# Moving step-size, read-out and copy instructions to other places in a scan loop that runs background work in slots

## The chip, the cores and the metric

The kernel runs on one core of a Trainium2 chip. Its engines are TensorE (PE in the profile, PEld for its weight loads), VectorE (DVE), ScalarE (ACT), GpSimd (POOL) and SyncE (SP), which issues all of the kernel's DMAs. Each engine works through its own list of instructions in order and waits for the others by semaphores. The metric is the device time of one execution in microseconds, and the median of several runs is compared.

## The reference, cut to what matters

Two residual layers work on 16 images of 64 x 64 pixels and 96 channels. The first layer upsamples by Fourier filters, applies a small network with a quadratic in the middle, and downsamples again. The second layer is a selective scan in four directions. Its core, per direction, is this recurrence over 4096 positions for 192 channels and 16 states each:

```python
delta = jax.nn.softplus(dts + dt_bias[None, :, :, None])
def step(h, inps):
    dt, ut, bt, ct = inps
    h = jnp.exp(dt[..., None] * As[None]) * h + (dt * ut)[..., None] * bt[:, :, None, :]
    y = jnp.einsum('bkdn,bkn->bkd', h, ct)
    return (h, y)
...
x = x + _L0_conv_ref(_gn(x), ...)
x = x + _L1_conv_ref(_gn(x), ...)
```

Both layers normalise their input by groups of channels over the whole image. Around the scan the second layer has a 3 x 3 convolution, projections that make `dt`, B and C, a layer norm, a gate and an output projection.

## The kernel before

**The loop.** `scan()` walks through 3072 units `(step, block, j)`: 16 images, 8 steps each (four stretches of T = 1024 positions forward with directions 0 and 1, then four backward with directions 2 and 3), 6 blocks per step (`blocks`, `bi` 0 to 5: 64 channels of one direction each), and 4 values of `j` (four states each). A tile has 32 channels x 4 states on its 128 partitions and 1024 positions along the free axis. A unit holds two such tiles, called odd (e = 1) and even (e = 0).

In each unit:

- ScalarE makes the decays, `da = exp(delta * A)`, in PSUM (`decay`, L821), one unit ahead.
- GpSimd makes `b = dtu * B` for both tiles (`drive`, L827), two units ahead.
- VectorE runs the recurrence of the odd tile, then of the even tile (`recur`, L836 forward and L838 backward), then multiplies the even states by C (L988).
- The odd states are multiplied by C on GpSimd (L977) for j = 0 to 2, and on VectorE (L968) for j = 3 (`odd_here`).
- `keep` (L844) copies the last state of each tile for the next stretch.
- TensorE sums over the states (`read_out`, L861, eight matmuls), one unit late: at unit n it reads out unit n-1. The result `y` gathers the four units of a block in one PSUM bank. In the backward half of an image, `y` begins with the forward part, fetched from DRAM and added by L853.
- After the last unit of a block, `store` copies `y` to SBUF on ScalarE (L872) and, one unit later, issues its DMA.

**Slots.** The order on each engine is written out by hand. Each unit calls `slot(0)`, `slot(1)` and `slot(2)` between its own instructions. A slot advances two generators by one piece: `work`, made by `block_work` for the block, and the background, if it is due. A block has 12 such places, p = 0 to 11, with p = 3j + position.

**The background** is `front(mi + 1)`, everything of the next image ahead of its scan, and after it `finish(mi - 1)`, everything of the last image behind its scan. A `Background` is due while its pieces so far are fewer than `at * SLICES / POS`, where POS = 576 is the number of places in an image. `front` says `WAIT` ahead of the activations that change ScalarE's table; they are then put into position 2 of a unit with j = 2. `norm` is called twice by `front`.

**The step sizes.** `block_work` also runs, once per block, a `task`. It makes 512 positions of `delta` and `dtu` for a later block. Its pieces in order are: fetch `u`, and a matmul into `s` (L683); Abs and Exp on ScalarE (L686, L687); Relu and `1 + e` (L689, L690); Ln (L692); `1 - w` (L694); one empty place; four matmuls that sum `w`, `e`, `d` and `m`, into `s` (L699); two or three empty places; `dtu = s * u` on VectorE (L703); a copy of `s` into `delta` on ScalarE (L705) and the DMA of `dtu` (L706); the DMA of `delta` (L708). Tasks in blocks 3 and 4 have `late = 1`: they begin one place later and make it up before L703, so the product is at place 9 in every block. In blocks 2 and 3 `block_work` also fetches three tiles of `u` at p = 6 and mixes them on TensorE at p = 11 (`mix`, L661); `mixed` turns the result into `pr` on ScalarE (L666) and stores its rows by DMA (L668) at p = 0 of the next block. `s` and `pp` share one PSUM bank, the only buffer of the pool `gps`. Of `y` there is one buffer, of `da` one per parity, of `b` four, of `u` four.

Of the kernel before, what the change touches and what calls it, by code (L numbers as in the profile page):

```python
# [64 lines left out]
NQ = 4  # L65
QT = T // NQ
TB = 512
# [1 line left out]
NEPS = 1e-5  # L69
BOTH = "natural_log_exp_and_others"  # L70
POS = 3 * 8 * 6 * NQ
SLICES = 540
FINISH = 117
WAIT = -1

# [2 lines left out]
def tile_two_blocks(  # L78
# [4 lines left out]
    nc = tc.nc  # L83
# [116 lines left out]
    def norm(xt):  # L200

        s = small.tile([C, 8], F32, name="gs")
        for t in range(8):
            junk = piece([C, TB], "junk")
            nc.scalar.activation(junk, xt[:, TB * t:TB * t + TB], AF.Identity, accum_out=s[:, t:t + 1])
            if t % 2:
                yield
        yield
        m_ps = bank([C, 8], "m_ps")
        nc.tensor.matmul(m_ps, lhsT=gmask_s, rhs=s, start=True, stop=True)  # L210
        yield
        junk8 = small.tile([C, 8], F32, name="junk8")
        nmean = small.tile([C, 1], F32, name="nmean")
        nc.scalar.activation(junk8, m_ps, AF.Identity, scale=-1.0, accum_out=nmean)
        s2 = small.tile([C, 8], F32, name="gs2")
        for t in range(8):
            junk = piece([C, TB], "junk")
            nc.scalar.activation(
                junk, xt[:, TB * t:TB * t + TB], AF.Square, bias=nmean, accum_out=s2[:, t:t + 1]
            )  # L220
            if t % 2:
                yield
        yield
        v_ps = bank([C, 8], "v_ps")
        nc.tensor.matmul(v_ps, lhsT=gmask_s, rhs=s2, start=True, stop=True)
        yield
        var = small.tile([C, 1], F32, name="var")
        nc.scalar.activation(junk8, v_ps, AF.Identity, accum_out=var)
        rg = small.tile([C, 1], F32, name="rg")
        nc.scalar.activation(var, var, AF.Ln, bias=eps_g[0:C])  # L230
        nc.scalar.activation(rg, var, AF.Exp, scale=-0.5)
        nb = small.tile([C, 1], F32, name="nb")
        nc.scalar.activation(nb, nmean, AF.Identity, scale=rg)
        yield
        yield
        return rg, nb
# [389 lines left out]
    def scan():  # L626


        with ExitStack() as es:
# [21 lines left out]
            def fetch_u(st, v, t):  # L651
                mi, _, lc = steps[st]
                uv = up_.tile([128, TB], F32, name="u")
                nc.sync.dma_start(out=uv, in_=image[mi]["xs"][v, :, lc * T + t:lc * T + t + TB])
                return uv

            def mix(st, us, ps):
                pair = steps[st][1]
                pp = ps.tile([128, TB], F32, name="pp", tag="g")
                for v in range(3):  # L660
                    nc.tensor.matmul(pp, lhsT=xpt_s[:, pair, v, :], rhs=us[v], start=(v == 0), stop=(v == 2))  # L661
                return pp

            def mixed(st, t, pp):
                pr = prp.tile([128, TB], F32, name="pr")
                nc.scalar.activation(pr, pp, AF.Identity, bias=bumps_s)  # L666
                for r in range(2):
                    nc.sync.dma_start(  # L668
                        out=ctxs[st]["rows"][r, :, t:t + TB], in_=pr[64 * r:64 * r + 2 * NS, :]
                    )  # L670
                ctxs[st]["pr"][t] = pr

            def task(st, k, ps, make, late=0):

                v, t = tasks[k]
                ctx, pair = ctxs[st], steps[st][1]
                u = fetch_u(st, v, t)
                for _ in range(late):  # L680
                    yield
                s = ps.tile([128, TB], F32, name="s", tag="g")
                nc.tensor.matmul(s, lhsT=dtw_s[:, pair, v, :], rhs=ctx["pr"][t], start=True, stop=True)  # L683
                yield
                e, d, m, w = (make(k) for k in ("e", "d", "m", "w"))
                nc.scalar.activation(e, s, AF.Abs)  # L686
                nc.scalar.activation(e, e, AF.Exp, scale=-1.0)  # L687
                yield
                nc.scalar.activation(m, s, AF.Relu)  # L689
                nc.scalar.activation(w, e, AF.Identity, bias=one_s)  # L690
                yield
                nc.scalar.activation(d, e, AF.Ln, bias=one_s)  # L692
                yield
                nc.scalar.activation(w, w, AF.Identity, scale=-1.0, bias=one_s)  # L694
                yield
                yield
                s = ps.tile([128, TB], F32, name="s", tag="g")
                for i, of in enumerate((w, e, d, m)):
                    nc.tensor.matmul(s, lhsT=ident_s, rhs=of, start=(i == 0), stop=(i == 3))  # L699
                for _ in range(3 - late):  # L700
                    yield
                dtu, delta = make("dtu"), make("delta")
                nc.vector.tensor_mul(dtu, s, u)  # L703
                yield
                nc.scalar.copy(delta, s)  # L705
                nc.sync.dma_start(out=ctx["dtu"][v][:, t:t + TB], in_=dtu)  # L706
                yield
                nc.sync.dma_start(out=ctx["delta"][v][:, t:t + TB], in_=delta)  # L708

            def near(name):  # L710
# [2 lines left out]
            def block_work(st, bi, mi):  # L713
                more = st + 1 < len(steps)
                work = iter(())
                if bi < 3:
                    work = task(st, bi + 3, gps, near)
                elif more:
                    work = task(st + 1, bi - 3, gps, near, 1 if bi < 5 else 0)
                for p in range(3 * NQ):  # L720
                    if p == 0 and more and bi in (3, 4):
                        mixed(st + 1, *mixing.pop())
                    next(work, None)
                    if more and bi in (2, 3):
                        if p == 6:
                            if bi == 2:
                                if steps[st + 1][0] > mi:
                                    ahead_gen.drain()
                                open_step(st + 1)
                            us = [fetch_u(st + 1, v, TB * (bi - 2)) for v in range(3)]  # L730
                        elif p == 11:
                            mixing.append((TB * (bi - 2), mix(st + 1, us, gps)))
                    yield

            def spread(out, what, ctx, bi, e):
# [33 lines left out]
            units = [(si_, bi, j) for si_ in range(len(steps)) for bi in range(len(blocks)) for j in range(NQ)]  # L769
# [37 lines left out]
            gps = es.enter_context(tc.tile_pool(name="sc_gps", bufs=1, space=PSUM))  # L807
# [10 lines left out]
            def decay(n, e):  # L818
                k, g = group(n, e)
                da = aps.tile([128, T], F32, name="da", tag=f"da{e}")  # L820
                nc.scalar.activation(da, deltas[n // NQ, e], AF.Exp, scale=a_s[:, k, g, units[n][2]:units[n][2] + 1])  # L821
                das[n, e] = da
# [88 lines left out]

            nothing = Background(None, 0, 1)
            ahead_gen = behind_gen = nothing
            work, mixing = iter(()), []

            def slot(position):
                back = ahead_gen if ahead_gen.gen is not None else behind_gen
                if back is behind_gen and back.at == 0:
                    back.positions = 3 * (per_image - n % per_image) - 6
                back.at += 1  # L920
                next(work, None)
                if back.due() and (back.said != WAIT or (position == 2 and units[n][2] == NQ - 2)):
                    back.step()
# [6 lines left out]
            storing = None  # L930

            for n, (st, bi, j) in enumerate(units):
# [11 lines left out]
                if j == 0:  # L944
                    work = block_work(st, bi, mi)
# [15 lines left out]
                odd_here = j == NQ - 1  # L961
                h = das[n, 1] if odd_here else bs[n][:, 1, :]
                recur(n, 1, h)
                if not odd_here:
                    decay(n + 1, 1)
                slot(0)
                if odd_here:
                    nc.vector.tensor_mul(bs[n][:, 1, :], h, bc[1, r, j])  # L968
# [3 lines left out]
                if storing is not None:  # L972
                    next(storing, 0)
                    storing = None
# [7 lines left out]
                recur(n, 0, h)  # L982
                if not odd_here:
                    keep(n, 1, states_of_odd, nc.vector.tensor_copy)
                if n >= 1:
                    read_out(n - 1)
                slot(1)
                nc.vector.tensor_mul(bs[n][:, 0, :], h, bc[1, r, j])  # L988
                keep(n, 0, h, nc.scalar.copy)
                if n < last:  # L990
                    decay(n + 1, 0)
                if n >= 1 and units[n - 1][2] == NQ - 1:
                    storing = store(n - 1)
                    next(storing)
                slot(2)
                if j == NQ - 1 and n < last and steps[units[n + 1][0]][1] == 1:
                    st2, bi2, _ = units[n + 1]
# [124 lines left out]
```

## Time and profile before

| | |
|---|---|
| median of the runs shown | 20482.93 us |
| lowest and highest | 20482.35, 20484.85 us |
| the profiled execution's own time | 20473.08 us |
| its span | 20471.3 us |
| granted clock of TensorE, mean | 0.873 |
| DMA engines' mean busy share in the loop, bytes per second | 0.66, 223 GB/s |
| L836 and L838, one scan with a carried state | 2340 to 2342 ns |
| L821, one decay | 1118 ns |
| L703, product of step size and u | 680 ns |
| L705, copy of delta | 579 ns |
| L872, copy of y | 579 ns |

The span is the time from the first instruction to the last of one profiled execution. A group's line gives the source line, the engine, the operation with what it writes and reads, the shapes, the count, the busy time, the mean duration of one, and the idle time just before them with what ended it. A line of waits gives who waited for whom, the total, the number of waits, and the longest. In a timeline, the first column is the start and the second the duration, both in us, and idle time stands in brackets at the end.

### The profile page before, as it was taken

Reading aid. Unit: us, or ns where it says so; the run is one execution under the profiler, and the core shown is the slowest. Engines: PE = TensorE matmul, PEld = TensorE weight load, DVE = VectorE, ACT = ScalarE, POOL = GpSimd, SP = SyncE. Lnnn points to the kernel's source line nnn. Section 1 sums busy time; section 2 is a strip of 40 time slices with the busy share of each in tenths; the row PEclk is TensorE's granted clock in tenths of the full one; section 3 lists DMA queues with packets and bytes.
Section 4 is the critical chain, followed back from the end, with each engine's and each line's share of the span. In section 5 each row is a group of like instructions: output and inputs, shape, how many; then the busy total and the mean of one; then the engine's idle time right before and its main releaser. Section 6 shows DMA issues by size and latency. Waiting matters only on the chain. (4 is left out here: it accounts for less than half of the span.)

```text
span 20471.3 us, 274485 instructions
## 1 busy us (share of the span) xinstructions
PE 16699.0 (82%) x98988; PEld 7171.0 (35%) x98988; DVE 19208.3 (94%) x12989; ACT 13815.5 (67%) x20694; POOL 19150.8 (94%) x5384
## 2 busy tenths in 40 slices
PE   7877888888888878788887888888887787888767
PEld 4423334343333433334233343433334333242222
DVE  0999999999999999999999999999999999999997
ACT  4676767667676776766767676676767767677554
POOL 0999999999999999999999999999999999999996
PEclk8888898988889889888888889888898888888888
DMA  2666666766667676666766667667676666766664
GB/s 85 212 224 208 223 234 211 242 214 222 231 218 239 210 240 220 217 235 214 235 218 221 234 215 238 218 220 234 217 237 210 234 223 216 238 217 232 221 214 157
DMA packets 1966064, 4478.55 MB, mean 219 GB/s; under 512 B 461726, under 2 KB 560958, under 8 KB 1962654
## 3 DMA queue, kind: packets, MB, share of 16 engines
q1 hardware_dynamic: 1964702, 4461.00, 64.5%
q8 instruction: 781, 12.80, 0.3%
q14 instruction: 581, 4.76, 0.1%
HBM read 3581.91 MB, written 878.18 MB: 218 GB/s over the span
## 5 line engine op out<-in xcount | busy, mean ns | idle before, releaser
L827 POOL TENSOR_TENSOR b<-dtu,bt 128x2048 f32<-128x2048 f32 x3072 | 13903.4, 4538 | 471.7 <-DMA dtu<-dtu_d 467.9
L821 ACT ACTIVATE da<-delta,a_s 128x1024 f32<-128x1024 f32 x6144 | 6868.4, 1118 | 2264.3 <-DVE b L988 849.7
L977 POOL TENSOR_TENSOR odd<-b,ct 128x1024 f32<-128x1024 f32 x2304 | 5456.2, 2368 | 679.3 <-DVE b L836 246.2
L988 DVE TENSOR_TENSOR b<-da,ct 128x1024 f32<-128x1024 f32 x3072 | 3760.5, 1224 | 41.8
L836 DVE TENSOR_TENSOR_SCAN da<-da,new,b 128x1024 f32<-128x1024 f32 x1440 | 3372.8, 2342 | 82.6 <-ACT da L821 78.9
L838 DVE TENSOR_TENSOR_SCAN da<-da,new,b 128x1024 f32<-128x1024 f32 x1440 | 3370.2, 2340 | 15.8 <-ACT da L821 14.7
L861 PE MATMUL y<-b,fold_s 128*32 128x256 f32 x30720 | 2561.2, 427 | 797.7 <-ACT yt L872 411.5
L844 ACT COPY new<-da 128x1 f32<-128x1 f32 x2880 | 457.1, 159 | 2434.9 <-DVE b L988 1892.3
L836 DVE TENSOR_TENSOR_SCAN b<-da,new,b 128x1024 f32<-128x1024 f32 x864 | 2023.8, 2342 | 29.3 <-ACT da L821 28.3
L838 DVE TENSOR_TENSOR_SCAN b<-da,new,b 128x1024 f32<-128x1024 f32 x864 | 2022.5, 2341 | 29.2 <-ACT da L821 29.2
L487 PE MATMUL c_ps<-xgp,wtap_s 96*64 96x512 f32 (+1 forms) x4608 | 1764.7, 640 | 77.7 <-ACT row L505 71.9
L861 PEld LDWEIGHTS y<-b,fold_s 128*32 128x32 f32 x30720 | 739.7, 114 | 2919.4 <-issue 1557.0
L861 PE MATMUL y<-odd,fold_s 128*32 128x256 f32 x18432 | 1599.9, 421 | 197.3 <-POOL odd L977 197.0
L683 PE MATMUL s<-pr,dtw_s 128*128 128x512 f32 x1536 | 1034.5, 761 | 689.9 <-ACT delta L705 574.0
L661 PE MATMUL pp<-u,xpt_s 128*128 128x512 f32 x1536 | 891.7, 726 | 461.4 <-ACT delta L705 319.1
L699 PE MATMUL s<-w,ident_s 128*128 128x512 f32 x1534 | 1054.0, 775 | 238.4 <-ACT w L694 211.5
L370 PE MATMUL h_ps<-xu,w1t_s 96*128 96x500 f32 x1920 | 1038.8, 642 | 166.1 <-ACT hsq L351 121.1
L836 DVE TENSOR_TENSOR_SCAN da<-da,b 128x1024 f32<-128x1024 f32 x480 | 1096.2, 2284 | 79.2 <-ACT da L821 75.1
L838 DVE TENSOR_TENSOR_SCAN da<-da,b 128x1024 f32<-128x1024 f32 x480 | 1095.2, 2282 | 10.7 <-ACT da L821 9.2
L382 PE MATMUL o_ps<-w2c_s,hsq 128*100 128x96 f32 x9600 | 1009.2, 263 | 71.6 <-ACT hsq L351 71.3
L382 PEld LDWEIGHTS o_ps<-w2c_s,hsq 128*100 128x100 f32 x9600 | 946.0, 176 | 266.2 <-ACT hsq L351 111.4
L487 PEld LDWEIGHTS c_ps<-xgp,wtap_s 96*64 96x64 f32 (+1 forms) x4608 | 631.8, 177 | 1081.2 <-issue 942.6
(140 smaller groups left out, 23002.7 us busy)
## 6 DMA issues: line engine op xcount, KB each, us to landing
dtu<-dtu_d SPq DMA_DIRECT2D x1536, 512.0 KB
delta<-delta_d SPq DMA_DIRECT2D x1536, 512.0 KB
bt<-rows SPq DMA_DIRECT2D x1024, 512.0 KB
ct<-rows SPq DMA_DIRECT2D x1024, 512.0 KB
u<-xs_d SPq DMA_DIRECT2D x1664, 256.0 KB
dtu_d<-dtu SPq DMA_DIRECT2D x767, 256.0 KB
delta_d<-delta SPq DMA_DIRECT2D x767, 256.0 KB
xr<-in_x SPq DMA_DIRECT2D x768, 128.0 KB
```

The source lines that it names most:

```text
L370: nc.tensor.matmul(h_ps[j], lhsT=w1t_s[:, 128 * j:128 * (j + 1)], rhs=xu.rearrange("c p q -> c (p q)"), start=True, stop=True,)
L382: nc.tensor.matmul(o_ps[:, p, :], lhsT=hsq[j][:, UPS * p:UPS * (p + 1)], rhs=w2c_s[:, j, :], start=(j == 0), stop=(j == HB - 1),)
L487: nc.tensor.matmul(c_ps[p:p + n], lhsT=wtap_s[:, tap, 128 * i:128 * i + n], rhs=xgp[:, h0:h0 + 8, dx:dx + HW], start=(tap == 0), stop=(tap ...
L683: nc.tensor.matmul(s, lhsT=dtw_s[:, pair, v, :], rhs=ctx["pr"][t], start=True, stop=True)
L699: nc.tensor.matmul(s, lhsT=ident_s, rhs=of, start=(i == 0), stop=(i == 3))
L821: nc.scalar.activation(da, deltas[n // NQ, e], AF.Exp, scale=a_s[:, k, g, units[n][2]:units[n][2] + 1])
L827: nc.gpsimd.tensor_mul(b, dtus[n // NQ], bt.unsqueeze(1).to_broadcast([128, 2, T]))
L836: nc.vector.tensor_tensor_scan(out, da, b, before, ALU.mult, ALU.add)
L838: nc.vector.tensor_tensor_scan(out[:, ::-1], da[:, ::-1], b[:, ::-1], before, ALU.mult, ALU.add)
L861: nc.tensor.matmul(y[32 * q:32 * q + 32, e, :], lhsT=fold_s, rhs=weighed[e][:, QT * q:QT * q + QT], start=(pair == 0 and j == 0 and e == 0 ...
L977: nc.gpsimd.tensor_mul(odds[n], h, bc[1, r, j])
L988: nc.vector.tensor_mul(bs[n][:, 0, :], h, bc[1, r, j])
```

## The change

- In `task`, `late` is gone. The four sums (L699) follow directly behind the piece with L694, at place 5, and four empty places stand between them and the product at place 9. The copy into `delta` stands in the same piece as the product; both DMAs stand together in the next piece.
- In `block_work`, the three `u` are fetched at p = 3, mixed at p = 10, and `mixed` is called at p = 11 of the same block.
- `read_out(n - 1)` stands ahead of `slot(0)` for j = 0 to 2. For j = 3 it stays behind the even scan.
- The first half of `store`, with the copy of `y`, stands behind `slot(1)`, ahead of the even product, the even `keep` and the even decay. Its DMA stays in the next unit.
- `norm` hands back after each of its activations, not after every second one. SLICES is 570, not 540.

```diff
-SLICES = 540
+SLICES = 570
...
             nc.scalar.activation(junk, xt[:, TB * t:TB * t + TB], AF.Identity, accum_out=s[:, t:t + 1])
-            if t % 2:
-                yield
+            yield
...
-            def task(st, k, ps, make, late=0):
+            def task(st, k, ps, make):
...
                 u = fetch_u(st, v, t)
-                for _ in range(late):
-                    yield
...
                 nc.scalar.activation(w, w, AF.Identity, scale=-1.0, bias=one_s)
                 yield
-                yield
                 s = ps.tile([128, TB], F32, name="s", tag="g")
                 for i, of in enumerate((w, e, d, m)):
                     nc.tensor.matmul(s, lhsT=ident_s, rhs=of, start=(i == 0), stop=(i == 3))
-                for _ in range(3 - late):
+                for _ in range(4):
                     yield
                 dtu, delta = make("dtu"), make("delta")
                 nc.vector.tensor_mul(dtu, s, u)
-                yield
                 nc.scalar.copy(delta, s)
+                yield
                 nc.sync.dma_start(out=ctx["dtu"][v][:, t:t + TB], in_=dtu)
-                yield
                 nc.sync.dma_start(out=ctx["delta"][v][:, t:t + TB], in_=delta)
...
-                    work = task(st + 1, bi - 3, gps, near, 1 if bi < 5 else 0)
+                    work = task(st + 1, bi - 3, gps, near)
                 for p in range(3 * NQ):
-                    if p == 0 and more and bi in (3, 4):
-                        mixed(st + 1, *mixing.pop())
                     next(work, None)
                     if more and bi in (2, 3):
-                        if p == 6:
+                        if p == 3:
...
                             us = [fetch_u(st + 1, v, TB * (bi - 2)) for v in range(3)]
+                        elif p == 10:
+                            pp = mix(st + 1, us, gps)
                         elif p == 11:
-                            mixing.append((TB * (bi - 2), mix(st + 1, us, gps)))
+                            mixed(st + 1, TB * (bi - 2), pp)
...
                 if not odd_here:
                     decay(n + 1, 1)
+                if n >= 1 and not odd_here:
+                    read_out(n - 1)
                 slot(0)
...
-                if n >= 1:
+                if n >= 1 and odd_here:
                     read_out(n - 1)
                 slot(1)
+                if n >= 1 and j == 0:
+                    storing = store(n - 1)
+                    next(storing)
                 nc.vector.tensor_mul(bs[n][:, 0, :], h, bc[1, r, j])
                 keep(n, 0, h, nc.scalar.copy)
                 if n < last:
                     decay(n + 1, 0)
-                if n >= 1 and units[n - 1][2] == NQ - 1:
-                    storing = store(n - 1)
-                    next(storing)
                 slot(2)
```

More of the change, by code (lines that the diff above doesn't have):

```diff
@@ L220, in norm @@
             )
-            if t % 2:
-                yield
+            yield
         yield
@@ L703, in task @@
                 nc.vector.tensor_mul(dtu, s, u)
+                nc.scalar.copy(delta, s)
                 yield
-                nc.scalar.copy(delta, s)
                 nc.sync.dma_start(out=ctx["dtu"][v][:, t:t + TB], in_=dtu)
-                yield
                 nc.sync.dma_start(out=ctx["delta"][v][:, t:t + TB], in_=delta)
@@ L913, in scan @@
             ahead_gen = behind_gen = nothing
-            work, mixing = iter(()), []
+            work = iter(())
             def slot(position):
```

## The prediction

> **What bounds the kernel now.** I read the page's busy shares first, then its costliest groups.
>
> ```profile
> span 20471.3 us, 274485 instructions
> ...
> PE 16699.0 (82%) x98988; PEld 7171.0 (35%) x98988; DVE 19208.3 (94%) x12989; ACT 13815.5 (67%) x20694; POOL 19150.8 (94%) x5384
> ...
> L827 POOL TENSOR_TENSOR b<-dtu,bt 128x2048 f32<-128x2048 f32 x3072 | 13903.4, 4538 | 471.7 <-DMA dtu<-dtu_d 467.9
> ...
> L977 POOL TENSOR_TENSOR odd<-b,ct 128x1024 f32<-128x1024 f32 x2304 | 5456.2, 2368 | 679.3 <-DVE b L836 246.2
> L988 DVE TENSOR_TENSOR b<-da,ct 128x1024 f32<-128x1024 f32 x3072 | 3760.5, 1224 | 41.8
> ```
>
> VectorE and GpSimd share the loop. It lasts from the first scan at 473.6 us to 20307.9, 19834 us for 768 blocks of four units. VectorE is busy 19183 us of it and idle 651. How far this can fall shows in two windows, images 14 and 15; the last runs no `front` for a following image.
>
> ```profile
> 17868.50:19108.00 1239.50, 1028.38 (x6186) 443.48 (x6186) 1199.93 (x811) 861.55 (x1294) 1197.08 (x337) 0.89 0.67 226
> 19108.00:20308.00 1200.00, 795.52 (x3945) 267.53 (x3944) 1194.55 (x801) 688.10 (x980) 1187.82 (x335) 0.78 0.59 205
> ```
>
> The columns are window, length, then PE, PEld, DVE, ACT and POOL busy. VectorE does the same work in both, but idles 40 us in the first and 5 in the second. So GpSimd doesn't hold the loop above 1200 us, and about 15 x 40 = 600 us are to be had. The waits of VectorE say from whom:
>
> ```profile
> DVE dtu L703 <- PE s L699: 455.1, 226, 159.9
> ...
> DVE da L836 <- ACT da L821: 154.0, 149, 3.5
> DVE b L838 <- ACT da L821: 88.2, 73, 2.4
> ```
>
> Of the 455, one wait of 159.9 lies ahead of the loop and a few more belong to it. Stepping through the timeline I count 286 us inside the loop, 236 of them (168 waits) in blocks 3 and 4, where `late=1`. The scans wait 322 us; 261 is the time by which a decay (L821) ended after VectorE was free: even scan of unit 1: 76; odd scan of unit 0: 67; even scan of unit 2: 60; odd scan of unit 2: 36; even scan of unit 3: 20. One of the stalled blocks on the merged timeline:
>
> ```profile
> 4616.15 1.08 PE L861 MATMUL y<-b,fold_s 128*32 128x256 f32 x8
> 4616.21 2.35 DVE L836 TENSOR_TENSOR_SCAN da<-da,new,b 128x1024 f32<-128x1024 f32 x1
> ...
> 4617.92 1.12 PE L699 MATMUL s<-w,ident_s 128*128 128x512 f32 x2
> ...
> 4620.60 1.02 PE L699 MATMUL s<-m,ident_s 128*128 128x512 f32 x2
> ...
> 4621.66 0.69 DVE L703 TENSOR_TENSOR dtu<-s,u 128x512 f32<-128x512 f32 x1 [3.10 <-PE s L699]
> ...
> 4623.24 0.56 ACT L310 COPY t<-o_ps 100x480 f32<-100x480 f32 x1 [5.60 <-PE o_ps L382]
> ...
> 4625.93 0.58 ACT L705 COPY delta<-s 128x512 f32<-128x512 f32 x1
> ```
>
> The four sums take 3.7 us on TensorE, come last in its queue, and both VectorE and ScalarE wait for them.
>
> **Part 1: sums one place forward, `late` gone.** Twelve places lie in a block, about 2.1 us apart. The sums move from place 6 to 5, in blocks 3 and 4 from 7 to 5; the product stays at 9. Where they had three places, 512 blocks lost 50 us in 56 waits; with two, 256 blocks lost 236, 1.4 us a wait. One or two places are 2 to 4 us more, above nearly every wait: I put 15 us for what is left, **-271 us**. The sums wait for `w` (place 4), which ScalarE ends 6.3 us into unit 1 on average; TensorE's work of that place ends at 7.6, so nothing new. With `late` go the Ln in place 4 and its followers in blocks 3 and 4, which hold back unit 2's decays: 31 us (odd) and 58 (even), against 7 in the four other blocks together. I leave 10: **-79 us**.
>
> **Part 2: delta copied right behind the product** (place 9 instead of 10). The single bank `g` comes free a place earlier:
>
> ```profile
> PE s L683 <- ACT delta L705: 574.0, 218, 5.0
> ...
> PE y L853 <- ACT yt L872: 341.2, 120, 6.4
> PE pp L661 <- ACT delta L705: 319.1, 123, 4.6
> ```
>
> Most of the first and third row goes. This is TensorE's time, with 18% idle; it pays only through what queues behind, and I count it in part 4. On the other side the copy now stands ahead of `keep` and the odd decay in unit 3. Here a rule speaks against the change. "PSUM — Partial Sum Buffer", section "PSUM bank collisions raise a hardware error", has two engines never touch one bank at once, so the copy must wait for the product. By the rule ScalarE stands still until 3.1 us into unit 3 (scan 2.34, product 0.68). By the trace it is free for this place at 3.4 us in the median and earlier in 49% of blocks, mean wait 0.8. Charging the wait in full to the decay would be 768 x 0.8 = 630 us. But `keep` and the decay wait anyway for L968, the instruction behind the product (1.21 us more), and the copy's 0.58 fits into it. Only where ScalarE is late already does 0.58 add: shifting each odd decay of unit 0 by 0.58 against its slack gives 109 us for 67. Ends 0 and +41; since the sums leave earlier, I take **+20 us**. On SyncE the dtu and delta stores now go out together at place 10; the one for dtu already holds the queue there, the one behind it waits less.
>
> **Part 3: `mix` at place 10, `mixed` at 11, u fetched at 3, front's norm halved.** Three u fetches go into SyncE's queue three places earlier; four buffers suffice, since the tile four fetches back was last read in the block before. The activation of pr (0.68 us) moves from ahead of the next unit 0's even decay to behind the previous one, and its two row stores into the end of the block, ahead of the next dtu fetch, with a unit's time in hand. It held the decay for 49 of the 76 us above; these are settled in part 4. `norm` hands back after one activation (0.81 to 0.90 us with its accumulator read) rather than two. By the yields `front` has 399 pieces instead of 383 and ends at position 460 of 576 instead of 448, `finish` still ends inside the image: nothing is drained in a burst. One 2.25 us stall per image (34 in all, odd scan of unit 0) follows the first silu; its place shifts by a block. Ends -34 and 0, I take **-15 us**.
>
> **Part 4: read-outs ahead of the background, y copied ahead of the even decay.** On TensorE a read-out takes 1.07 us and comes, in units 0 to 2, before instead of behind the first place's matmuls. Its odd product is there: GpSimd ends it 0.7 us before unit 1 begins and 0.1 us into unit 2. What is queued behind it is dt's matmul (1.1 us) or background; for those ScalarE waits in the second place, ahead of the even decay. That decay is the tight one: L988 ends 5.85 us into the unit, the next odd scan 2.34 later, `keep` and decay take 0.16 + 1.12, so ScalarE must be through at 6.9. In unit 0 the chain is now: TensorE free at B, read-out 1.07, s 1.1, Abs and Exp 1.22, y copy 0.58: B + 4.0; with background on both engines about B + 5.5. It is late where B exceeds 2.9, or 1.4. B follows from where TensorE's work of the block before ends: median 0.1, 90% point 3.8 us in blocks 0 and 1; in 3 and 4, with pp at place 10 for 2.7 us, above 3 in a quarter. Block by block this gives 170 us of late even decays in unit 1 where the trace has 76. The same addition in the old order gives 36 for blocks 0, 1, 2 and 5, where the trace has 27. Halved norms ease 20: **+74 us**. Units 1 and 2 in the same way: 9 and 49 us, less where TensorE had idled: **+50 us**. The y copy leaves ScalarE's second half of unit 0 and frees y for the next read-out (the middle row above); its DMAs don't move. GpSimd's queue keeps its order.
>
> **Sum.** -271 - 79 + 20 - 15 + 74 + 50 = -221 us. The profiled run took 20473.1 us, its span 20471.3; the median shown is 10 us above. 20483 - 221 = 20262, rounded to **20260 us**.
>
> **Rivals.** (a) Likeliest, 0.57: as summed, 20100 to 20420. (b) The read-out costs nothing, since B falls too once `s` and pp no longer wait for delta (for it: the 574 and 319 us; against: B is mostly background). Then part 4 is about -60 instead of +124, and the loop nears the last image's pace: -405, about 20080, down to 19950. Chance 0.25. (c) Slower: ScalarE waiting at Abs behind the read-out in unit 0 takes the place of the old stalls. It decides through B: at B + 1 my addition gives 250 us, at B + 2 421, at B + 3 891. The gain is gone a little beyond B + 2; at B + 2.5 it is some 650, +260 in all: 20740. For it: the sums stand earlier, and the background that they displace comes later in the block. Against: TensorE's whole work doesn't grow. Chance 0.12. (d) The earlier sums merely wait for `w`, and the stalls move from L703 to the decays, about 20480: 0.06. Against it is 7.6 beyond 6.3.
>
> **The numbers.** The ends of the unknowns (15 to 50 left at L703, 0 to 41, 0 to 34, -60 to +250) give -444 to -24, 20040 to 20460; I draw the lower end down to 20000 to take in most of (b). A change within 0.2% (41 us) can't be told from none here. Faster 0.80, within it 0.07, slower 0.13.
>
> **What would show it.** L703's waits for L699 fall from 226 to below 60. The waits of `s` and pp for delta shrink to a third. Scans of unit 2 in blocks 3 and 4 stop waiting. Abs waits longer for s (now 51.6 us), and the waits of the scans for L821 stay near 300 us, shifted to the even scan of unit 1. If they exceed 550, I am wrong through (c); below 170, through (b). GpSimd's busy time stays at 19150.

## The result, and the profile after

The changed kernel takes 20740.95 us in the median (20737.66 to 20749.26), against 20482.64 for the kernel before on the same chip: a ratio of 1.0127, 95% interval 1.0109 to 1.0144. The forecast was 20260 us, with 20000 to 20460 as its range. The profiled span is 20747.5 us, 276 more than before.

The lines numbered L827, L977, L988, L836, L838, L821, L699, L703 and L705 before are L821, L973, L987, L830, L832, L815, L694, L698 and L699 now. First the page of the changed kernel, its busy shares and costliest groups.

```profile
span 20747.5 us, 275259 instructions
...
PE 16745.8 (81%) x98988; PEld 7167.9 (35%) x98988; DVE 19210.8 (93%) x12989; ACT 13789.8 (66%) x20694; POOL 19150.4 (92%) x5384
...
L821 POOL TENSOR_TENSOR b<-dtu,bt 128x2048 f32<-128x2048 f32 x3072 | 13904.7, 4538 | 527.0 <-DMA dtu<-dtu_d 470.1
...
L973 POOL TENSOR_TENSOR odd<-b,ct 128x1024 f32<-128x1024 f32 x2304 | 5448.0, 2365 | 897.5 <-DVE b L832 283.9
```

The two engines that share the loop do no more work: VectorE is busy 19210.8 us against 19208.3, GpSimd 19150.4 against 19150.8. The whole difference is waiting. VectorE's idle time inside the loop grew from 651 to 920 us. Its waits, as before with the total, the number and the longest:

```profile
DVE da L830 <- ACT da L815: 370.5, 308, 3.6
...
DVE da L832 <- ACT da L815: 257.5, 163, 3.8
DVE yz L577 <- ACT sq L564: 204.4, 33, 31.0
DVE dtu L698 <- PE s L694: 169.1, 15, 159.0
DVE yz L588 <- ACT sq L583: 51.5, 36, 3.9
```

The product's waits for the sums fell from 226 to 15, and all but 10 us of what is left lies ahead of the loop. That is the intended gain. Two things took its place: the scans wait for decays, and the products of `finish` (L577 and L588) wait inside the loop, which they hardly did. Sorting VectorE's waits in the loop by what waited gives this table, in us:

| wait of VectorE | before | forecast | after |
|---|---|---|---|
| product of the step size, for the sums | 286 | 15 | 10 |
| odd scan of unit 0 | 78 | 83 | 0 |
| scans of unit 2, both | 118 | 112, together with the even scan of unit 3 | 54 |
| even scan of unit 1 | 84 | 158 | 276 |
| even scan of unit 3 | 23 | in the row of unit 2 | 238 |
| even scan of unit 0 | 1 | 1 | 61 |
| products of `finish` | 5 | 5 | 206 |

Most of the last line, 136 of 206 us, is one event in each of the 14 images that have a `front` and a `finish`: the first product of `finish`. On the timeline of the changed kernel, TensorE, ScalarE and VectorE in turn, in image 5:

```profile
7775.90 2.08 PE L555 MATMUL yc<-y,pmat_s 128*128 128x512 f32 x2 [11.47 <-DMA y<-y_d]
```
```profile
7785.82 0.60 ACT L564 ACTIVATE sq<-yc 128x512 f32<-128x512 f32 x1 [12.41 <-PE yc L568]
```
```profile
7786.45 0.69 DVE L577 TENSOR_TENSOR yz<-yc,z 128x512 f32<-128x512 f32 x1 [9.82 <-ACT sq L564]
```

TensorE stands 11.5 us for the first y of `finish`, ScalarE 12.4 for TensorE, and VectorE 9.8 for ScalarE. The square itself takes 0.60 of VectorE's 9.82: the page names ScalarE as the releaser because it came last, and at the head of the chain stands the DMA of y. The windows of the changed kernel around it, with the columns of the windows shown before, and the granted clock, the DMA engines' busy share and GB/s at the end:

```profile
7733.70:7739.50 5.80, 3.94 (x18) 1.10 (x18) 5.80 (x6) 4.97 (x7) 5.80 (x3) 0.65 1.03 330
7739.50:7758.50 19.00, 14.21 (x63) 5.24 (x64) 18.96 (x14) 10.27 (x16) 19.00 (x6) 0.73 1.02 375
7758.50:7775.00 16.50, 2.79 (x20) 0.71 (x18) 14.69 (x11) 10.54 (x16) 16.04 (x5) 0.70 1.03 335
7775.00:7797.70 22.70, 21.80 (x81) 7.38 (x82) 11.56 (x11) 5.12 (x8) 11.87 (x4) 0.84 0.74 229
```

For 41 us the DMA engines are full. TensorE works 2.8 of the third window's 16.5 us, and VectorE 11.6 of the fourth's 22.7.

### The profile page after: what moved, and what is told of

It is laid out like the page before. It is cut to its first block, busy times and chain, and to the rows that moved or that the text cites. A ratio compares the mean times of both kernels' runs of the same rounds, so it can differ in the third digit from the quotient of the medians.

```text
span 20747.5 us, 275259 instructions
## 1 busy us (share of the span) xinstructions
PE 16745.8 (81%) x98988; PEld 7167.9 (35%) x98988; DVE 19210.8 (93%) x12989; ACT 13789.8 (66%) x20694; POOL 19150.4 (92%) x5384
## 5 line engine op out<-in xcount | busy, mean ns | idle before, releaser
L821 POOL TENSOR_TENSOR b<-dtu,bt 128x2048 f32<-128x2048 f32 x3072 | 13904.7, 4538 | 527.0 <-DMA dtu<-dtu_d 470.1
L815 ACT ACTIVATE da<-delta,a_s 128x1024 f32<-128x1024 f32 x6144 | 6849.6, 1116 | 1950.3 <-DVE b L987 813.5
L973 POOL TENSOR_TENSOR odd<-b,ct 128x1024 f32<-128x1024 f32 x2304 | 5448.0, 2365 | 897.5 <-DVE b L832 283.9
L987 DVE TENSOR_TENSOR b<-da,ct 128x1024 f32<-128x1024 f32 x3072 | 3759.6, 1224 | 42.3
L830 DVE TENSOR_TENSOR_SCAN da<-da,new,b 128x1024 f32<-128x1024 f32 x1440 | 3374.1, 2343 | 301.1 <-ACT da L815 299.8
L832 DVE TENSOR_TENSOR_SCAN da<-da,new,b 128x1024 f32<-128x1024 f32 x1440 | 3371.6, 2341 | 201.4 <-ACT da L815 201.4
L830 DVE TENSOR_TENSOR_SCAN b<-da,new,b 128x1024 f32<-128x1024 f32 x864 | 2023.4, 2342 | 12.5 <-ACT da L815 12.5
L832 DVE TENSOR_TENSOR_SCAN b<-da,new,b 128x1024 f32<-128x1024 f32 x864 | 2022.2, 2340 | 0.0
L694 PE MATMUL s<-w,ident_s 128*128 128x512 f32 x1534 | 1121.3, 821 | 706.9 <-ACT w L690 703.6
L855 PE MATMUL y<-odd,fold_s 128*32 128x256 f32 x18432 | 1531.1, 405 | 137.4 <-POOL odd L973 136.9
L838 ACT COPY new<-da 128x1 f32<-128x1 f32 x2880 | 460.3, 160 | 1770.3 <-DVE b L987 1684.0
L659 PE MATMUL pp<-u,xpt_s 128*128 128x512 f32 x1536 | 965.3, 778 | 304.0 <-ACT new L838 206.7
L830 DVE TENSOR_TENSOR_SCAN da<-da,b 128x1024 f32<-128x1024 f32 x480 | 1095.9, 2283 | 79.7 <-ACT da L815 70.7
L832 DVE TENSOR_TENSOR_SCAN da<-da,b 128x1024 f32<-128x1024 f32 x480 | 1095.2, 2282 | 57.4 <-ACT da L815 56.1
L679 PE MATMUL s<-pr,dtw_s 128*128 128x512 f32 x1536 | 1086.0, 796 | 71.9 <-ACT pr L664 66.4
L694 PE MATMUL s<-e,ident_s 128*128 128x512 f32 x1534 | 1030.8, 762 | 0.0
```

The source lines that it names most:

```text
L821: nc.gpsimd.tensor_mul(b, dtus[n // NQ], bt.unsqueeze(1).to_broadcast([128, 2, T]))
L830: nc.vector.tensor_tensor_scan(out, da, b, before, ALU.mult, ALU.add)
L832: nc.vector.tensor_tensor_scan(out[:, ::-1], da[:, ::-1], b[:, ::-1], before, ALU.mult, ALU.add)
L855: nc.tensor.matmul(y[32 * q:32 * q + 32, e, :], lhsT=fold_s, rhs=weighed[e][:, QT * q:QT * q + QT], start=(pair == 0 and j == 0 and e == 0 ...
L973: nc.gpsimd.tensor_mul(odds[n], h, bc[1, r, j])
```

## The experiments

Three theories stood at the start. T1: `finish` begins at a bad place. T2: the read-outs ahead of the background hold ScalarE up. T3: the early sums do. All medians below stand beside the kernel before at 20482 to 20487 us on the same chip. Differences of some 20 us between two runs are within their scatter.

**e1: SLICES 585.** `front` ends at place 448 again.

```diff
-SLICES = 570
+SLICES = 585
```

> The changed kernel with SLICES 585, so that front again ends at place 448 of an image and finish begins 12 places earlier, as before. Theory T1 (the first y fetch of finish falls behind pr's row stores in SyncE's queue and TensorE stands 11 us at yc, once per image): the waits of VectorE at the two yz products and the last product of finish inside the loop fall from 206 us to under 40, and the time from 20741 to about 20550. Rivals T2 (read-outs ahead of the background hold ScalarE ahead of the even decay) and T3 (the sums ahead of the background do): that wait is not the cause, the time stays within 40 us of 20741.

20250.62 us, ratio 0.9888 (0.9872 to 0.9904). The waits of finish's products fell from 206 to 42, as T1 has it; but the even scans' waits fell as well, from 628 to 352, and the time by 490 where 190 were expected. One constant turns the change from a loss into the forecast gain. T1 is too narrow.

**e2: read-outs and y copy in their old places**, the rest as changed.

```diff
-                if n >= 1 and not odd_here:
-                    read_out(n - 1)
                 slot(0)
...
-                if n >= 1 and odd_here:
+                if n >= 1:
                     read_out(n - 1)
                 slot(1)
-                if n >= 1 and j == 0:
-                    storing = store(n - 1)
-                    next(storing)
...
                     decay(n + 1, 0)
+                if n >= 1 and j == 0:
+                    storing = store(n - 1)
+                    next(storing)
                 slot(2)
```

> The changed kernel with read-outs and the y copy in their old places, all else as changed. T2: the even scans' waits of unit 1 fall from 276 to about 100 us and of unit 3 from 238 to about 50, the time to about 20390. T3: they stay above 400 together, and the time above 20650. The waits of finish's products stay near 200 us under both.

20543.46 us, ratio 1.0028 (1.0017 to 1.0039). Unit 1's even scans fell to 55, as T2 had it; unit 3's stayed at 217, which it had not. The new places of read-outs and y copy cost 197 us here, but without them the kernel is still slower than before.

**e3: the new task and the new places of the u fetches, mix and mixed alone**; e2's edit, and `norm` (both of its loops) and SLICES as before.

```diff
             nc.scalar.activation(junk, xt[:, TB * t:TB * t + TB], AF.Identity, accum_out=s[:, t:t + 1])
-            yield
+            if t % 2:
+                yield
...
-SLICES = 570
+SLICES = 540
```

> The kernel before with the new task and the new places of the u fetches, mix and mixed alone; read-outs, y copy, norm and SLICES as before. T2: the gain at L703 (276 us) and at the late decays is kept, about 20150 to 20300. T3: even scans of units 1 and 3 wait over 400 us together, about 20480 to 20560.

20226.07 us, ratio 0.9876 (0.986 to 0.9892). T3 falls: the early sums alone bring 256 us. Between e3 and e2 lies nothing but the background's part, and it is 317 us.

**e4: the y copy behind the even decay again**, the last hunk of e2's edit.

> The changed kernel with the y copy behind the even decay again. If the y copy's 0.58 us ahead of the even decay is a large part of the loss, the even scans' waits of unit 1 fall by 100 us or more and the time to 20640 or less. If T2 or T3 hold without it, the time stays within 50 us of 20741.

20756.41 us, ratio 1.0135 (1.0116 to 1.0154): within the scatter of the changed kernel, so the y copy isn't the loss.

**e5: norm and SLICES as before, the rest as changed** (e3's diff on the changed kernel).

> The changed kernel with norm and SLICES (540) as before, all the rest as changed: the background part alone is undone. Theory P (where front's pieces fall among the twelve places of a block, and where finish begins, makes the loss; the read-outs cost what they cost in any case): the read-out and y part cost 197 us with SLICES 570 (20741 against 20543), so 20226 + 197, about 20420. Theory Q (the read-outs only cost much under an unlucky fall of the pieces): about 20250, as with SLICES 585. Theory R (the background part is innocent, and SLICES 585 was a chance gain): 20741.

20269.4 us, ratio 0.9896 (0.9881 to 0.9911). R falls, and it is nearer Q than P: read-outs and y copy cost 43 us with this background and 197 with the other.

**e6: SLICES 585 with e2's edit.**

> SLICES 585 with read-outs and y copy in their old places. P: 197 us below SLICES 585 with the new places, about 20050. Q: within 60 us of 20250.

20159.29 us, ratio 0.9842 (0.9826 to 0.9859). Between P and Q: the read-outs and the y copy cost 91 us here. This is the lowest median of all runs.

**e7: the halved norm (both loops) and SLICES 570 alone on the kernel before.**

```diff
-SLICES = 540
+SLICES = 570
...
-            if t % 2:
-                yield
+            yield
```

> The kernel before with the halved norm and SLICES 570 alone. P: the background part adds about what it adds to the new task (20543 against 20226, 317 us), with the old late sums as they were: 20700 to 20850, and the first product of finish waits about 9 us per image. R: 20440 to 20520.

20797.45 us, ratio 1.0153 (1.0137 to 1.0168). The background part alone costs 310 us, where it cost 317 with the new task. Read the other way, the new task and mix gain 254 us with this background (e7 to e2) and 256 with the old one (e3). The first product of `finish` waits 138.7 us in 14 images, 9.9 each, and the late sums 439 instead of 286.

**e8: finish fetches its first y and u ahead of the y columns.**

```diff
-        yield from parts(ycol[0], y_d[1, 0:128, :])
-        yield from parts(ycol[1], y_d[1, 128:DI, :], 2)
-
         def fetch_y(t):
...
         ahead = fetch_y(0)
+        yield from parts(ycol[0], y_d[1, 0:128, :])
+        yield from parts(ycol[1], y_d[1, 128:DI, :], 2)
```

> The changed kernel with finish's first fetch of y and u ahead of its six fetches of y columns, five places earlier, so not behind pr's row stores. If TensorE's wait for that y is what holds VectorE at the first product of finish, its 136 us inside the loop go, and the time falls by 120 to 180 us to about 20590. If the first y only takes part of the blame, by under 60.

20728.72 us, ratio 1.0121 (1.0106 to 1.0136): 12 us, within the scatter, and not 120. TensorE's timeline of e8, image 5, shows why. That y is there now, and the next transfer is late instead, the forward part of y for the read-out, and with it VectorE's wait at the same product stays at 87 of 136 us:

```profile
7756.81 1.51 PE L554 MATMUL yc<-y,pmat_s 128*128 128x512 f32 x2
...
7766.24 2.05 PE L846 MATMUL y<-y,ident_s 128*128 128x512 f32 x2 [6.20 <-DMA y<-part]
```

That part of y is used 8.9 us after its issue in the mean of 14 images, and TensorE stands for it in each. So one fetch moved in SyncE's order doesn't help; the one behind it comes late in its place.

**e9: SLICES 571 instead of 570.** A piece is due while `n * 576 < at * SLICES`. The first `WAIT` of `front` is piece 293. With 570 it comes at place 296, with 571 at 295. The activations behind it may only go into position 2 of a unit with j = 2, which place 296 is. Reached at 295, the place is used; reached at 296, they wait for place 308, and `front` ends at 460 instead of 448.

```diff
-SLICES = 570
+SLICES = 571
```

> The changed kernel with SLICES 571 instead of 570. front says its first WAIT at place 295 instead of 296 of an image, so its first silu goes into place 296 and not 308, front ends at 448 and finish begins 12 places earlier; ahead of place 295 nothing of note moves. Theory D (the missed place, and with it finish's loads falling on those of B and C, is the cause): the scans' waits in places 0 to 290 of an image stay near 400 us, those behind fall from 460 to about 160, and the time to about 20430. Rival P (the fall of the pieces in the first 290 places counts, as SLICES 585 against 570 had it): within 100 us of 20741.

20385.94 us, ratio 0.9954 (0.9939 to 0.9969): **355 us for one count**. VectorE's waits from place 460 on fell from 326 to 64 us, 136 of it at the first product of `finish`, between 290 and 460 they stayed (148 and 153), and ahead of place 290 they fell from 399 to 310, where the expectation had none. TensorE in e9, at the first y of an image:

```profile
7614.45 2.07 PE L679 MATMUL s<-pr,dtw_s 128*128 128x512 f32 x2
7617.36 1.12 PE L555 MATMUL yc<-y,pmat_s 128*128 128x512 f32 x2 [0.84 <-DMA y<-y_d]
```

The wait of 11.47 is 0.84. The windows of e9 around it show that the DMA engines are as full here as there:

```profile
7593.40:7612.40 19.00, 12.03 (x58) 4.21 (x58) 18.96 (x14) 10.29 (x16) 19.00 (x6) 0.68 1.01 367
7612.40:7638.20 25.80, 24.53 (x103) 7.95 (x104) 25.80 (x20) 15.19 (x23) 25.80 (x8) 0.92 1.03 323
```

What differs is when in a step it falls. In e9 `finish` starts in the sixth unit of a step, and its six y columns and its first y are issued ahead of the loads of B and C (`fetch_bc`, eighth to twelfth unit). In the changed kernel it starts in the tenth, and four of these loads stand between its first y column and its first y. SyncE's timeline, the changed kernel and then e9, has that y at

```profile
7767.31 0.34 SPq L533 DMA_DIRECT2D y<-y_d  x1
```
```profile
7609.42 0.58 SPq L533 DMA_DIRECT2D y<-y_d  x1
```

In the changed kernel TensorE has stood free for it since 7764.4, before it is issued; in e9 TensorE comes to it 7 us after the issue. From issue to use it takes about as long in both, 9.3 and 8.5 us in the mean of 14 images. So in this pair the load isn't slower, SyncE issues it later. In image 5 SyncE waits 1.7 us ahead of that issue, until a load of B lands (`SPq L533 <- DMA bt<-rows`). That the loads of B and C are what holds SyncE up is argued from this and from the order; no run moved them alone.

**e10: the kernel before with SLICES 539 instead of 540**, the mirror of e9: the first `WAIT` moves from place 295 to 296.

```diff
-SLICES = 540
+SLICES = 539
```

> The kernel before with SLICES 539 instead of 540 and nothing else. By the same count its first WAIT moves from place 295 to 296 and front's end from 448 to 460. D: 200 to 300 us slower, 20680 to 20790, with about 9 us at the first product of finish per image. P, or a cause in the halved norm: 20450 to 20520.

20874.06 us, ratio 1.0195 (1.018 to 1.021): 392 us slower, with neither the halved norm nor any reordering. D has the direction of e9 and e10 right and their sizes too small: it gave 310 and 200 to 300 us. VectorE in e10:

```profile
DVE dtu L703 <- PE s L699: 694.6, 288, 160.0
...
DVE yz L579 <- DMA z<-z_d: 121.6, 12, 11.4
```

Its waits behind place 460 are 368 us where the kernel before has 124; the first product of `finish` waits 10.0 us in each of 14 images. Here the first y is issued almost as early as in the kernel before (3.1 us ahead of TensorE's coming for it, against 3.6), and the load takes longer, 12.0 us from issue to use against 8.2. Ahead of place 290 the waits rose too, from 369 to 509, although only single pieces moved there, by one place. All of that rise is the product waiting for the late sums.

**e11 and e12: read-outs ahead in units 1 and 2 alone, and in unit 0 alone**, both with SLICES 585. e11 keeps the y copy's old place, e12 the new one. The diff is e11's; e12 has `j == 0` and `j != 0` in these lines.

```diff
-                if n >= 1 and not odd_here:
+                if n >= 1 and j in (1, 2):
...
-                if n >= 1 and odd_here:
+                if n >= 1 and j not in (1, 2):
```

> SLICES 585, read-outs ahead of the background in units 1 and 2 alone, read-out of unit 0 and y copy in their old places. Theory U0 (what the read-outs cost is the read-out in unit 0 ahead of s and Abs; in units 1 and 2 they gain): even scans of unit 1 wait below 40 us, odd scans of unit 3 about 17, 20055 to 20110. Rival (units 1 and 2 cost the 50 us that the forecast had): 20190 or more.

> SLICES 585, read-out ahead of the background and y copy ahead of the even decay in unit 0 alone; units 1 and 2 read out in their old places. U0: even scans of unit 1 wait about 210 us, 20300 to 20370. Rival: 20150 to 20210.

20176.78 us (ratio 0.9851, 0.9835 to 0.9868) and 20209.17 us (0.9863, 0.9849 to 0.9878), against 20159 with neither and 20251 with both. U0 has the place right: even scans of unit 1 wait 15 us in e6, 23 in e11 and 155 in e12, 152 of these in blocks 3 and 4. But in e12 scans of unit 3 win back 72 (206 to 135), so its price is 50 us and not 180, and one of e12's four runs took 20161; and in units 1 and 2 the read-outs change the time by 18 us, within the scatter, where U0 had a gain. U0's times are missed in both runs, and neither order is a gain.

All with the new task and the new places of the mix, medians in us:

| background | old read-outs and y copy | new |
|---|---|---|
| as before (540) | 20226 | 20269 |
| halved norm, 570 | 20543 | 20741 (the change) |
| halved norm, 585 | 20159 | 20251 |

## Why the prediction was wrong

**Parts 1 and 2 (the sums, delta)** and the mix were right in mechanism and near in size. The product's waits fell by 276 us (forecast 271), scans of unit 2 by 64 (forecast 79). (In the stalled block that the prediction shows, the sums were not last in TensorE's queue: ScalarE's 5.60 us end with `o_ps`, whose matmuls stand behind them.) The copy of delta does wait for the product, and TensorE's wait for it shrank as announced, the one of pp from 319 us, by the changed kernel's waits of ScalarE and TensorE:

```profile
ACT delta L699 <- DVE dtu L698: 440.7, 290, 6.8
```
```profile
PE pp L659 <- ACT delta L699: 85.7, 67, 2.1
```

The charge of +20 for this on the odd scan of unit 0 did not come: that scan waits 69 us in e3 against 78 before. That its wait is gone in the changed kernel is not the sums' doing, since with the same sums e5 has 53 and e9 52. In e3's profile, 228 us shorter than the kernel before's (256 in the medians), the three terms come to -336 where -330 was forecast; the even scans of unit 3 (from 23 to 89 us) and the products of `finish` (from 5 to 38), which no term held, give most of the difference back.

**Part 4 (read-outs, y copy)** was charged +124. Measured are +43, +91 and +197, by the background beside it. The late even decays of unit 1 in blocks 3 and 4 are real: 273 of the 276 us in the changed kernel's row of unit 1 lie there. The chain that part 4 gives for them fits: Abs waits for `s` 320 us in e12, with the read-out ahead in unit 0 alone, and in the changed kernel and in e6, by ScalarE's waits:

```profile
ACT e L682 <- PE s L679: 297.4, 313, 2.6
```
```profile
ACT e L682 <- PE s L679: 38.4, 101, 0.8
```

With the background left as it was, the sum of parts 1, 2 and 4 is -206; e5, which is that with the new places of the mix, stands at -218. That agreement is luck: parts 1 and 2 were forecast at -330 and gave -256, part 4 at +124 and gave +43.

**Part 3 failed**, in the sentence that `front` "has 399 pieces instead of 383 and ends at position 460 of 576 instead of 448, `finish` still ends inside the image: nothing is drained in a burst". The count was right and its price wasn't taken. I looked for a burst at the image's end and for the stall of the first silu, which "shifts by a block", and put down -15 us. The term measures +310 on the kernel before (e7), +317 with the new task (e3 to e2) and +471 with everything else changed (e5 to the change). Places 448 and 460 differ because one `WAIT` missed its only allowed place by one. A forecast that saw a number move by 12 should have asked what forces steps of 12, and what else lies at the new place: the loads of B and C, three u fetches and the stores of pr. The windows of the kernel before show the DMA engines full at finish's start already (share 1.01):

```profile
7622.20:7641.20 19.00, 11.47 (x60) 3.88 (x60) 18.97 (x14) 10.64 (x16) 19.00 (x6) 0.77 1.01 374
```

What the runs show in its place is that this one step of 12 places costs 355 to 392 us (e9, e10), and where the waits then stand: behind place 460 they are 262 us more in the changed kernel than in e9. Another 89 us lie ahead of place 290, and their cause stays open.

**Rival (c)** named 20740 us and would have been confirmed by the sign it gave, scans waiting more than 550 us for decays (they wait 648 us). Yet e2 removes its mechanism and leaves the kernel slower than before, and e9 and e5 remove the loss and leave its mechanism in place. The number agrees by chance; (c) accounts for 197 us at most of what the change lost, and for 43 with the background as it was. (Its 421 us at B + 2 make the sum a loss of some 30 already, not a little beyond B + 2.) The expected reordering gain was there and was given back.

Open: which pieces make the 90 to 140 us ahead of place 290, where a shift of single pieces by one place is all that e9 and e10 change. Open too is the other 135 us between e9 (20386) and SLICES 585 (20251), which both end `front` at 448. The halved norm itself was not run alone; e7 is 77 us faster than e10, which ends `front` at the same place without it, so nothing speaks for it as the loss.

## What to carry to other kernels

Where work is dealt out by a rule like `n * positions < at * slices` and some pieces may only go into certain places, list the place of every such piece before and after a change: a piece that misses its place by one waits for the next one, and everything behind it moves. Then ask which loads and products the moved work now meets. Measure such a constant at several values before a reordering is judged with it, for here it decides between 20251 and 20741 us for the same order; and the reordering to keep is the one that gains by the same amount under each background that it was tried with, the early sums (256 us with the old one, 254 with the halved norm and 570), with the read-outs left where they were. With SLICES 585 that is the fastest run, 20159 us; the late sums were not run with 585.

## What the runs showed of the hardware that was not expected

- With all 16 DMA engines full (share 1.01 to 1.03, 323 to 375 GB/s), a load of 256 KB was used 8.5 to 9.3 us after its issue in e9 and in the changed kernel, TensorE standing for it each time, and 12.0 us after it in e10. Moving one transfer up in the issuing queue gave 12 us, within the scatter, of the 136 at stake; a wait of 6.2 us turned up at the next transfer.
- The granted clock of TensorE was 0.871 after and 0.873 before, so a lower clock isn't the change's loss. Over all the profiles it lay between 0.860 and 0.883, 0.862 in e10 and 0.877 in e9; whether it has a share in those differences no run separates.
